# Conditioned two-stage block on one core: statistics of the first eight batch rows taken ahead, wider slot rows, and a new place for the third and fourth slot tile

## The chip, the core and the metric

The kernel runs on one core of a Trainium2 chip. The core has five engines with an instruction stream each: TensorE (PE, matmuls; its weight loads are a row of their own, PEld), VectorE (DVE), ScalarE (ACT), GpSimd (POOL) and SyncE (SP), which here only issues transfers. Each stream is executed in its own order and waits on semaphores. ACT and POOL issue transfers too; the instruction that issues one occupies the engine's stream. The metric is the device time of one execution in microseconds (us).

## The reference

All data is float32. The inputs are `x` (32 batch rows of 128 tokens of 512 features), a condition `t` (32 x 512), a mask (32 x 128) and the weights.

```python
shift, scale, gate = split(silu(t) @ ada_w + ada_b, 3)
norm = layernorm(x) * (1 + scale) + shift, zero where not mask
x = x + gate * where(mask, fwd(norm) + bwd(norm), 0)      # each: gelu(u @ w1 + b1) @ w2 + b2
shift2, scale2, gate2 = split(silu(t) @ ffada_w + ffada_b, 3)
ff = gelu_tanh((layernorm(x) * (1 + scale2) + shift2) @ ff_w1 + ff_b1) @ ff_w2 + ff_b2
out = x + gate2 * ff
```

The two halves of the first stage act on each token alone, so they are one product with a hidden layer of 1024. The mask is set for the *padding*, at most a quarter of the tokens, so the first stage is needed for few tokens.

## The kernel before, in words

**First stage on slots.** The masked tokens are packed into 512 slots, four tiles of 128 (`xc[0]` to `xc[3]`). Their numbers come from small matmuls on the mask (`find_slots`, L250), and POOL gathers their rows of `x` (`gather_slots`, L254). Each slot's scale, shift and gate are rows of a small matrix `mod1` (32 rows each), spread to the slots by matmuls of 32 x 512 (`slot_part`, L288): part 1 is scale, part 0 shift, part 2 gate. `mod1` itself comes from `modulation_matmuls` (L260) on the transposed condition. A slot tile is normalised and modulated on VectorE (`statistics` L149, `modulated` L166), transposed by TensorE and copied back by ScalarE (`transposed_slots`, L175). Tiles 0 and 1 together go through the hidden layer (`hidden`, L182: eight blocks of 4 matmuls with 256 columns, each ended by a GELU on ScalarE) and through the output layer (`project`, L196, one call for each tile); then `finish_slots` (L296) adds bias, gate and `x` and stores the rows into the DRAM scratch `x1_rows`. Tiles 2 and 3 follow in the same way at L1155 to L1200.

**Second stage on all tokens.** The 32 batch rows are taken in four pairs of sides; a pair is eight batch rows, a side four. For pair 0, `x` is loaded whole (L520), then `take_first_half` (L670) lets POOL gather the finished slot rows from `x1_rows` over the masked tokens, one indirect transfer per batch row; unmasked tokens keep `x`. Then come layernorm statistics (`Statistics`, L693), normalising, and a transposition: of side 0 by VectorE in 32 x 32 blocks and by 16 transfers (`turned`, L738) with ScalarE scaling afterwards (`scaled`, L747); of side 1 by TensorE (`transposed`, L730), called between the matmuls of `project` of tile 3. Both feed-forward products are done with seven block products in place of eight (`FirstProduct` L813, `SecondProduct` L1014), for which VectorE forms sums of weight blocks (`Weights.combine` L313, `weight_sums` L568) and of token blocks (`TokenBlocks.one`, L768). Some weight sums are stored in DRAM (`store_weight_sums`, L580) and loaded again (`load_weights`, L847). After pair 0's first matmul (L1210) the pairs run one after the other, and the next pair's gathers and statistics are put between the matmuls of the present one.

**What sets the order.** From L360 to L1362 the order in each stream is written by hand (`manual_schedule`): program order is stream order. SP's loads are issued in the order of the text: `ada_w` (3 MB), `w1` (2 MB) and `w2` (2 MB) behind the first gathers (L473 to L476), `ff_w1` (2 MB), `ffada_w` (3 MB), the broadcast biases, `ff_w2` (2 MB) and last `x` of pair 0 (2 MB, L520). On VectorE, between the statements named above, stand `count_more` (L585), the four combines of `ff_w1` (L620), `weight_sums` 1, 2, 3 and 4 (L624, L628, L633, L667) and the combines of `ff_w2` (L635).

## Time and profile before

| | us |
|---|---|
| median of three runs | 464.28 |
| lowest and highest | 462.79, 465.20 |
| profiled execution: span from its first to its last instruction | 463.6 |
| TensorE busy | 448.9 (97%) |
| VectorE busy | 330.6 (71%) |
| ScalarE busy | 175.7 (38%) |
| GpSimd busy | 159.8 (34%) |
| first hidden-layer matmul of slot tiles 0 and 1 (L188) | at 20.93 |
| last matmul of `project` of tile 1 ends (L203) | at 51.99 |
| first hidden-layer matmul of tiles 2 and 3 (L188) | at 57.94 |
| first matmul of pair 0's first product (L906) | at 87.27 |
| first matmul of the second product (L1093) | at 133.01 |

The page of the profile gives busy time by engine, the span in 40 slices of 11.6 us, and the costliest groups of instructions. The timeline of an engine lists its instructions in order; behind an instruction stands in brackets how long the engine sat idle before it, and what ended that. A float32 matmul with full precision is two instructions in these lists: `po_s` of L203, one `project`, is 8 matmuls and shows as x16. Matmuls overlap their successors, so their listed length is longer than the distance between two starts (592 ns against 430 ns for 512 columns, 379 ns against 216 ns for 256).

### The profile page before, as it was taken

The numbers are of one execution on the slowest core, as the hardware profiler recorded it, in microseconds if no ns is written. First come the engines' busy times: TensorE is split into PE (matmuls) and PEld (weight loads), VectorE is DVE, ScalarE is ACT, GpSimd is POOL, SyncE is SP. The second block draws the span as 40 slices with busy tenths as digits, with TensorE's granted clock in tenths as the row PEclk, the third lists the DMA queues.
The fourth block names the chain that finished last, engine by engine and source line by source line (L and its number), as shares of the span: only waits on it lengthen the run. The fifth ranks groups of instructions, "written<-read, shape, count | busy, mean of one in ns | idle before, by whom it ended". The sixth has DMA issues, their size and how long they took to land.

```text
span 463.6 us, 5827 instructions
## 1 busy us (share of the span) xinstructions
PE 448.9 (97%) x2000; PEld 364.4 (79%) x2000; DVE 330.6 (71%) x538; ACT 175.7 (38%) x380; POOL 159.8 (34%) x153
## 2 busy tenths in 40 slices
PE   6899999998999999999999999999999999999995
PEld 2475385676788888888888888888888887888884
DVE  4649778998669739996787498957963985433645
...
GB/s 280 386 408 364 322 107 95 219 326 104 85 5 211 97 102 105 354 90 113 1 229 113 68 169 310 99 81 34 212 105 60 155 142 79 81 74 109 0 81 105
DMA packets 82419, 70.42 MB, mean 152 GB/s; under 512 B 63168, under 2 KB 63696, under 8 KB 81362
## 3 DMA queue, kind: packets, MB, share of 16 engines
...
## 4 chain that ended last, share of the span: by engine, by line
PE 72%; DVE 8%; DMA 5%; SPq 4%; POOL 4%; issue 3%; ACT 3%; POOLq 0%; ACTq 0%; DVEq 0%
PE a_o L1093 17%; PE a_m L906 14%; PE e_o L1093 13%; PE e_m L906 11%; PE ph_s L188 6%; PE po_s L203 6%; SPq L745 4%; DMA x<-in_x_dram 2%; POOL x L674 1%; DMA xc<-in_x_dram,token_i_s 1%; DMA tw<-t_rows 1%; ACT xT L728 1%; PE part_s L283 1%; POOL ha L957 1%; PE pm_f L263 1%
## 5 line engine op out<-in xcount | busy, mean ns | idle before, releaser
L957 POOL TENSOR_TENSOR ha<-p_m,ha 128x512 f32<-128x512 f32 x20 | 26.2, 1311 | 151.9 <-ACT ha L964 142.0
L1093 PE MATMUL e_o<-fw,ha 128*128 128x256 f32 x256 | 57.9, 379 | 0.0
L728 ACT ACTIVATE xT<-xT,modT 128x128 f32<-128x128 f32 x112 | 44.0, 480 | 31.9 <-DMA xT<-xn 31.9
L1093 PE MATMUL a_o<-t,hb 128*128 128x256 f32 x240 | 54.1, 379 | 0.0
L1093 PEld LDWEIGHTS e_o<-fw,ha 128*128 128x128 f32 x256 | 48.6, 190 | 6.6
L1093 PEld LDWEIGHTS a_o<-t,hb 128*128 128x128 f32 x240 | 45.6, 190 | 6.2
L674 POOL DMA_INDIRECT x<-x_rows,slot_i x32 | 38.1, 1192 | 30.1 <-DMA x_rows<-t_s 18.0
L868 ACT ACTIVATE hb<-hb,biasT 128x256 f32<-128x256 f32 x64 | 29.0, 500 | 29.1 <-POOL hb L990 19.3
L957 POOL TENSOR_TENSOR hb<-p_m,hb 128x512 f32<-128x512 f32 x20 | 29.3, 1464 | 18.9 <-DVE sx L835 18.6
L920 ACT COPY p_m<-e_m 128x512 f32<-128x512 f32 x27 | 15.8, 586 | 47.9 <-PE e_m L906 47.9
L964 ACT COPY ha<-e_m 128x512 f32<-128x512 f32 x32 | 18.5, 578 | 28.6 <-PE e_m L906 26.6
L931 DVE TENSOR_TENSOR e_m<-a_m,ha 128x512 f32<-128x512 f32 x20 | 14.0, 698 | 21.6 <-POOL ha L957 9.5
L188 PE MATMUL ph_s<-xT_s,w 128*128 128x256 f32 x128 | 28.6, 381 | 0.5 <-issue 0.5
L1093 PE MATMUL a_o<-t,s 128*128 128x256 f32 x128 | 28.9, 379 | 0.0
L1093 PE MATMUL a_o<-fw,ha 128*128 128x256 f32 x128 | 28.9, 379 | 0.0
L1093 PE MATMUL e_o<-fw,s 128*128 128x256 f32 x128 | 28.9, 379 | 0.0
L203 PE MATMUL po_s<-w,h_s 128*128 128x512 f32 x64 | 28.6, 592 | 0.0
L188 PEld LDWEIGHTS ph_s<-xT_s,w 128*128 128x128 f32 x128 | 24.0, 190 | 5.2 <-ACT h_s L192 1.5
L1093 PEld LDWEIGHTS a_o<-t,s 128*128 128x128 f32 x128 | 24.3, 190 | 3.3
L1093 PEld LDWEIGHTS e_o<-fw,s 128*128 128x128 f32 x128 | 24.3, 190 | 3.3
L1093 PEld LDWEIGHTS a_o<-fw,ha 128*128 128x128 f32 x128 | 24.3, 190 | 3.3
L868 ACT ACTIVATE ha<-e_m,biasT 128x256 f32<-128x256 f32 x48 | 20.1, 468 | 16.2 <-PE e_m L906 10.5
...
## 6 DMA issues: line engine op xcount, KB each, us to landing
...
```

Source lines behind the costliest of these rows:

```text
L188: nc.tensor.matmul(ph[:, :n], w[:, k, ts(f, P)], xT[:, k, :], start=(k == 0), stop=(k == KC - 1))
L203: nc.tensor.matmul(po, h[f][:, ts(i, P)], w[:, f, :], start=(f == 0), stop=(f == HC - 1))
L674: nc.gpsimd.indirect_dma_start(out=xs[i // G][i % G // 2][:, i % 2], out_offset=None, in_=x1_rows[:slots, :], in_offset=bass.IndirectOffse ...
L728: nc.scalar.activation(out, src, AF.Identity, bias=shift, scale=scale)
L745: queues[b % len(queues)].dma_start(dst[ts(q, R), b], src[ts(b, R), q])
L868: nc.scalar.activation(dst[:, n], src[:, n], AF.Gelu_apprx_tanh, bias=biasT[:, f : f + 1])
L906: nc.tensor.matmul(bank[:, ts(n, QT)], self.w_block(j, product)[:, ts(n, P)], self.x_block(j, product), start=(product in ("P1", "P5") and ...
L920: nc.scalar.copy(p5, e)
L931: nc.vector.tensor_tensor(e, a, p5, add)
L957: nc.gpsimd.tensor_tensor(self.place(RESULT[j], c), self.p5[j], other, ALU.add)
L964: nc.scalar.copy(self.place(RESULT[j], c), src)
L1093: nc.tensor.matmul(part, src[:, k, ts(i, P)], w[product][:, k, :], start=(last and k == 0), stop=True, skip_group_check=True,)
```

## The change

It does the following.

- *Opening.* The bias of `mod1` and the bias rows of the hidden layers are loaded from ScalarE's queue in place of POOL's. The slots of tiles 2 and 3 are found before the last of the four blocks of the scale and shift matmuls. The gate part of `mod1` is computed as four independent products side by side in one bank, which are then added up by one more matmul with a 0/1 matrix (`strips`). Tiles 0 and 1 have statistics of their own each, and the first three hidden blocks are computed for tile 0 (128 columns) before tile 1 is transposed, then for tile 1.
- *Loads.* `x` of pair 0 goes ahead of `w2`, the two output biases of the first stage ahead of `ff_w1`.
- *Statistics ahead.* The tiles of `x` of pair 0 are two columns wider; VectorE writes mean and 1/deviation of each token there (`own_statistics`), POOL the power. The rows that `finish_slots` stores for tiles 0 and 1 carry the same two columns, into a second scratch `x1_wide`, and pair 0's gathers read from it. `Statistics` is not used for pair 0 any more.
- *Bias and x joined.* For tiles 0 and 1, `x + gate * bias` is formed ahead (`with_gated_bias`), so `finish_slots` has one multiplication and one addition before its statistics.
- *Tiles 2 and 3.* Their scale and shift rows, their modulation and their transposes go from between the first hidden blocks to behind `project` of tile 1, beside the modulation of the second stage; their gates go between the first and second hidden block of tiles 2 and 3.
- *VectorE's order.* `weight_sums` 1 and 2 go behind that too, normalising of side 0 to hidden block 4, `weight_sums(4)` and the normalising of side 1 to block 7, the combines of `ff_w2` and `fb2_step` behind the token block sum. The transfers of `turned` are issued in four groups between hidden blocks, each spread over both queues, and TensorE's transposes of side 1 stand in `project` of tile 2.

```diff
+    def own_statistics(t, n, name):
+        for i in range(n):
+            st = stp.tile([P, 6], F32, tag="st", name=f"st_{name}_{i}")
+            row = t[:, i]
+            nc.vector.bn_stats(st, row[:, :D])
+            nc.vector.bn_aggr(row[:, D : D + 2], st)
+        var = t[:, :, D + 1]
+        nc.vector.tensor_scalar(var, var, EPS, None, ALU.add)
+        nc.gpsimd.tensor_tensor(var, var, half[:, :n], ALU.pow)
...
+            for g in (after or {}).get(f, ()):
+                g()
...
+    def with_gated_bias(at, gate):
+        t = tp.tile([P, D], F32, tag="t", name=f"bg_s_{at}")
+        nc.vector.tensor_tensor(t, b2, gate, ALU.mult)
+        nc.vector.tensor_tensor(xc[at], xc[at], t, ALU.add)
     def finish_slots(at, h1, gate):
-        t = gated(project(at % (NC // 2), h1, w2, f"s{at}"), b2, gate, f"s_{at}")
-        nc.vector.tensor_tensor(t, t, xc[at], ALU.add)
-        nc.sync.dma_start(x1_rows[ts(at, P), :], t)
+        t = tp.tile([P, 1, D + 2], F32, tag="t", name=f"t_s_{at}")
+        row = t[:, 0, :D]
+        nc.vector.tensor_tensor(row, project(at, h1, w2, f"s{at}"), gate, ALU.mult)
+        nc.vector.tensor_tensor(row, row, xc[at], ALU.add)
+        own_statistics(t, 1, f"s_{at}_x1")
+        nc.sync.dma_start(x1_wide[ts(at, P), :], t[:, 0])
+        nc.sync.dma_start(x1_rows[ts(at, P), :], row)
...
-    broadcast_rows(modb_a, ada_b, nc.gpsimd)
     half = const.tile([P, G], F32, name="half")
     nc.vector.memset(half, -0.5)
+    strips = ssm.tile([P, B], F32, name="strips")
+    nc.vector.tensor_reduce(
+        strips, ident.rearrange("p (a b) -> p b a", b=B), axis=AX.X, op=ALU.add
+    )
...
+    broadcast_rows(modb_a, ada_b, nc.scalar)
...
-    load_behind_gathers(w1[:, :, :D], ssm_w1)
-    load_behind_gathers(w1[:, :, D:], bwd_w1)
-    load_behind_gathers(w2[:, :KC], ssm_w2)
-    load_behind_gathers(w2[:, KC:], bwd_w2)
-        nc.gpsimd.dma_start(
+        nc.scalar.dma_start(
...
-    modulation(pm, mod1, ada_a, modb_a, 0, 2)
-    gather_slots(find_slots(1, (ps_h, "h")))
-    rows = [(slot_part(c, 1, ps_o, "o"), slot_part(c, 0, ps_h, "h")) for c in range(2)]
-    pm = ps_o.tile([P, 512], F32, tag="o", name="pm_g")
...
-    mv, rstd = statistics(xc[:2], "s01")
-    xn_s = [
-        modulated(
-            xc[c], *rows[c], f"s{c}", xn[:, c], (mv[:, c, 0:1], rstd[:, c : c + 1])
-        )
-        for c in range(2)
-    ]
-    modulation_matmuls(pm, ada_a, 2, 3, range(KC))
...
-    for t, vec in ((b2, ssm_b2), (b2b, bwd_b2), (modb_f, ffada_b), (fb2, ff_b2)):
-        broadcast_rows(t, vec, nc.sync)
-    nc.sync.dma_start(fw2, ff_w2.rearrange("(k p) f -> p k f", p=P))
-    x_of = {0: load_x(0)}
-    transposed_slots(xn_s[0], xT_s[:, :, ts(0, P)], "s0")
-    transposed_slots(xn_s[1], xT_s[:, :, ts(1, P)], "s1")
...
+    gather_slots(find_slots(0))
+    load_behind_gathers(w1[:, :, :D], ssm_w1)
+    load_behind_gathers(w1[:, :, D:], bwd_w1)
+    raw = [x_tile(2 * n, 2) for n in range(2 * G // 2)]
+    x_of = {0: [[t[:, :, :D] for t in raw[2 * side : 2 * side + 2]] for side in range(2)]}
+    for n, t in enumerate(raw):
+        nc.sync.dma_start(t[:, :, :D], x[2 * n : 2 * n + 2].rearrange("b s d -> s b d"))
+    load_blocks(w2[:, :KC], ssm_w2)
+    load_blocks(w2[:, KC:], bwd_w2)
+    pick_slots(1)
...
+    modulation_matmuls(pm, ada_a, 0, 2, range(KC - 1))
+    gather_slots(find_slots(1, (ps_h, "h")))
+    modulation_matmuls(pm, ada_a, 0, 2, range(KC - 1, KC))
+    modulation_rows(pm, mod1, modb_a, 0, 2)
+    rows = [(slot_part(c, 1, ps_o, "o"), slot_part(c, 0, *((ps_o, "o"), (ps_h, "h"))[c])) for c in range(2)]
...
+    xn_s = [modulated(xc[c], *rows[c], f"s{c}", xn[:, c]) for c in range(2)]
...
+    for t, vec in ((b2, ssm_b2), (b2b, bwd_b2)):
+        broadcast_rows(t, vec, nc.sync)
+    nc.sync.dma_start(fw1, ff_w1.rearrange("(k p) f -> p k f", p=P))
+    ada_f = load_ada(ffada_w, "f", 3 * D)
+    for t, vec in ((modb_f, ffada_b), (fb2, ff_b2)):
+        broadcast_rows(t, vec, nc.sync)
+    nc.sync.dma_start(fw2, ff_w2.rearrange("(k p) f -> p k f", p=P))
...
+        if c == 0:
+            ph_s[f] = ps_h.tile([P, 512], F32, tag="h", name=f"ph_s0_{f}")
+        for k in range(KC):
+            nc.tensor.matmul(
+                ph_s[f][:, ts(c, P)],
+                w1[:, k, ts(f, P)],
+                xT_s[:, k, ts(c, P)],
+                start=(c == 0 and k == 0),
+                stop=(k == KC - 1),
+                skip_group_check=True,
...
+    transposed_slots(xn_s[0], xT_s[:, :, ts(0, P)], "s0")
+    gate_parts = tp.tile([P, D], F32, tag="t", name="gate_parts")
+    pm = ps_o.tile([P, 512], F32, tag="o", name="pm_g")
+    for k in range(KC):
+        nc.tensor.matmul(
+            pm[ts(k, B), :], sT[:, k, :], ada_a[:, k, ts(2, D)], start=True, stop=True
+        )
+    nc.scalar.copy(gate_parts, pm)
...
+    hidden_of_tile(0, 0)
+    pm = ps_o.tile([P, 512], F32, tag="o", name="pm_gate")
+    nc.tensor.matmul(pm[ts(2, B), :], strips, gate_parts, start=True, stop=True)
+    modulation_rows(pm, mod1, modb_a, 2, 3)
+    hidden_of_tile(1, 0)
+    transposed_slots(xn_s[1], xT_s[:, :, ts(1, P)], "s1")
+    hidden_of_tile(2, 0)
...
+    total, start_at, more_i, col_l = count_more()
+    for n, t in enumerate(raw):
+        own_statistics(t, 2, f"x_{n}")
     h1 = []
-    gs = []
-    xn_s = []
-    for c in range(2):
-        h1 += hidden(xT_s, NH, w1, 0, AF.Gelu, "s0", ssm, range(4 * c, 4 * c + 3))
-        if c == 0:
-            total, start_at, more_i, col_l = count_more()
-        gs.append(keep_gate(c, slot_part(c, 2, ps_o, "o")))
-        rows = slot_part(2 + c, 1, ps_o, "o"), slot_part(2 + c, 0, ps_o, "o")
-        xn_s.append(modulated(xc[2 + c], *rows, f"s{2 + c}", xn[:, 2 + c]))
-        if c == 0:
-            Weights(fw1, KC // 2, FF // 2, t_1).combine(0, 1, 2, 3)
-        h1 += hidden(xT_s, NH, w1, 0, AF.Gelu, "s0", ssm, range(4 * c + 3, 4 * c + 4))
-        if c == 1:
-            transposed_slots(xn_s[0], xT_t[:, :, ts(0, P)], "s2")
-    weight_sums(1)
+    for f in range(3):
+        hidden_of_tile(f, 1)
+        t = ssm.tile([P, NH], F32, tag="h", name=f"h_s0_{f}", bufs=HC)
+        nc.scalar.activation(t, ph_s[f][:, :NH], AF.Gelu, bias=biasT[:, f : f + 1])
+        h1.append(t)
+    gs = [keep_gate(c, slot_part(c, 2, ps_o, "o")) for c in range(2)]
+    mv_t, rstd_t = statistics(xc[2:], "s23")
     nc.vector.tensor_tensor(b2, b2, b2b, ALU.add)
     b2_row = dram.tile([1, D], F32, name="b2_row")
-    nc.sync.dma_start(b2_row, b2[0:1, :])
-    weight_sums(2)
+    for c in range(2):
+        with_gated_bias(c, gs[c])
+    Weights(fw1, KC // 2, FF // 2, t_1).combine(0, 1, 2, 3)
+    h1 += hidden(xT_s, NH, w1, 0, AF.Gelu, "s0", ssm, range(3, HC))
     finish_slots(0, h1, gs[0])
-    transposed_slots(xn_s[1], xT_t[:, :, ts(1, P)], "s3")
     t = in_blocks(group_of_tiles("tw_3"))
     t_sum[3] = [t[:, :4], t[:, 4:]]
     weight_sums(3)
...
+    store_weight_sums(3)
     nc.vector.tensor_scalar(modb_f[B : 2 * B], modb_f[B : 2 * B], 1.0, None, ALU.add)
     finish_slots(1, h1, gs[1])
-    store_weight_sums(3)
+    nc.sync.dma_start(b2_row, b2[0:1, :])
+    rows = [(slot_part(2 + c, 1, ps_o, "o"), slot_part(2 + c, 0, ps_h, "h")) for c in range(2)]
...
-    modulation(pm, mod2, ada_f, modb_f, 0, 3)
+    modulation_matmuls(pm, ada_f, 0, 3, range(KC))
+    xn_late = ssm.tile([P, 2, D], F32, tag="xT", name="xn_s_late", bufs=2)
+    for c in range(2):
+        t = modulated(
+            xc[2 + c], *rows[c], f"s{2 + c}", xn_late[:, c], (mv_t[:, c, 0:1], rstd_t[:, c : c + 1])
+        )
+        transposed_slots(t, xT_t[:, :, ts(c, P)], f"s{2 + c}")
+    modulation_rows(pm, mod2, modb_f, 0, 3)
...
-    gs = [
-        keep_gate(2, slot_part(2, 2, ps_o, "o")),
-        keep_gate(3, slot_part(3, 2, ps_h, "h")),
-    ]
+    weight_sums(1)
...
-    ptr = ps_t.tile([P, 512], F32, tag="tr", name="ptr_mod")
...
+    def transposed_modulation():
...
+    def second_gates():
+        gs[:] = [
+            keep_gate(2, slot_part(2, 2, ps_o, "o")),
+            keep_gate(3, slot_part(3, 2, ps_o, "o")),
+        ]
...
-    nc.vector.tensor_tensor(fb2_step, fb2[:, D // 2 :], fb2[:, : D // 2], ALU.subtract)
-    weight_sums(4)
+    fw2_of = Weights(fw2, HC // 2, D // 2, t_2)
...
+                out=raw[i // 2][:, i % 2] if p == 0 else xs[i // G][i % G // 2][:, i % 2],
                 out_offset=None,
-                in_=x1_rows[:slots, :],
+                in_=x1_rows if p else x1_wide,
...
-        for b in range(P // R):
+        for b in which:
             for q in range(P // R):
-                queues[b % len(queues)].dma_start(dst[ts(q, R), b], src[ts(b, R), q])
+                queues[(b + q // 2) % len(queues)].dma_start(dst[ts(q, R), b], src[ts(b, R), q])
...
-    take_first_half(0, x_of[0], range(G + 1))
-    store_weight_sums(1, queue=nc.gpsimd)
-    stats = [Statistics(x_of[0][side], f"0_{side}") for side in range(2)]
+    take_first_half(0, x_of[0], range(2 * G))
+    store_weight_sums(1)
     xT = [new_xT(0, side) for side in range(2)]
-    for i in range(G):
-        stats[0].one(i)
-    stats[0].root()
-    take_first_half(0, x_of[0], range(G + 1, 2 * G))
...
-    for i in range(G):
-        t = stats[0].normalised(i, xn[:, :, i])
-        nc.vector.transpose(t, t)
-    h1 = hidden(xT_t, NH, w1, 0, AF.Gelu, "s1", ssm)
-    turned(xn, xT[0], (nc.sync, nc.scalar))
+    def normalised_of_side_0():
+        for i in range(G):
+            t = normalised(raw[i // 2][:, i % 2], xn[:, :, i])
+            nc.vector.transpose(t, t)
...
+    def normalised_of_side_1():
+        t = sp.tile([P, G, D], F32, tag="s12", name="xn_0_1")
+        for i in range(G):
+            xn_b.append(normalised(raw[2 + i // 2][:, i % 2], t[:, i]))
...
+    def turn_rows(b):
+        return lambda: turned(xn, xT[0], (nc.sync, nc.scalar), (b,))
+    after = {4 + b: [turn_rows(b)] for b in range(4)}
+    after[0] = [second_gates, transposed_modulation]
+    after[1] = [lambda: weight_sums(2)]
+    after[4].insert(0, normalised_of_side_0)
+    after[7] += [lambda: weight_sums(4), normalised_of_side_1]
+    h1 = hidden(xT_t, NH, w1, 0, AF.Gelu, "s1", ssm, after=after)
     nc.scalar.activation(warm, biasT[0:1, 0:1], AF.Gelu_apprx_tanh)
     for k in range(KC):
         scaled(0, xT[0], k)
-    for i in range(G):
-        stats[1].one(i)
-    stats[1].root()
-    xn_b = []
-    for c in range(2):
...
-    po_s2 = project(0, h1, w2, "s2")
...
-    between = {0: turn(0), 1: turn(1), 2: keep_and_turn, 4: turn(3)}
-    po = project(1, h1, w2, "s3", between, (ps_h, "h"))
-    store_weight_sums(4, 2)
+    po_s2 = project(0, h1, w2, "s2", {2: turn(0), 4: turn(1), 6: turn(2), 7: turn(3)})
     of_x[0] = TokenBlocks(0, xT)
     of_x[0].one(1)
+    fw2_of.combine(0, 1)
+    nc.vector.tensor_tensor(fb2_step, fb2[:, D // 2 :], fb2[:, : D // 2], ALU.subtract)
+    with_bias(2, po_s2)
+    with_gate(2, gs[0])
+    with_x(2)
+    po = project(1, h1, w2, "s3", bank=(ps_h, "h"))
+    store_weight_sums(4, 2)
     with_bias(3, po)
     with_gate(3, gs[1])
```

## The prediction

> **What bounds the kernel now.** I read the page first, then TensorE's timeline up to 135 us, VectorE's for the same stretch, and last who waits for whom behind pair 0's first product. Parts 1 and 2 of the page:
>
> ```profile
> PE 448.9 (97%) x2000; PEld 364.4 (79%) x2000; DVE 330.6 (71%) x538; ACT 175.7 (38%) x380; POOL 159.8 (34%) x153
> ...
> PE   6899999998999999999999999999999999999995
> ```
>
> TensorE is the bound nearly everywhere. Only slices 0 and 8 and the tail have room, so an edit pays only if it takes TensorE's own work away, or idle time in those places. TensorE's timeline of the opening (start, length, idle before it):
>
> ```profile
> 12.86 1.99 PE L283 MATMUL part_s<-mod,pick 32*128 32x512 f32 x8 [0.15 <-DVE mod L273]
> 14.78 3.62 PE L263 MATMUL pm_g<-ada_a,sT 128*32 128x512 f32 x8
> 18.33 0.66 PE L179 MATMUL ptr_s<-ident,xn_s 128*128 128x128 f32 x4
> 19.55 0.66 PE L179 MATMUL ptr_s<-ident,xn_s 128*128 128x128 f32 x4 [0.56 <-DVE xn_s L172]
> ...
> 20.93 5.42 PE L188 MATMUL ph_s<-xT_s,w 128*128 128x256 f32 x24 [0.49 <-issue]
> ...
> 34.48 1.13 PE L283 MATMUL part_s<-mod,pick 32*128 32x512 f32 x6
> ...
> 52.08 3.63 PE L263 MATMUL pm_f<-ada_f,sT 128*32 128x512 f32 x24
> 55.64 1.98 PE L283 MATMUL part_s<-mod,pick 32*128 32x512 f32 x4
> ```
>
> From 20.93 to 98 us the timeline lists no idle time over 0.3 us. Two things matter. The gate product (14.78) is done while the slot rows are still on their way, so it costs nothing now. And a gate, scale and shift that stand together share 1.13 us (34.48: three matmuls on different rows of the array, side by side), while two gates alone take 1.98 us (55.64: same rows, one after the other).
>
> VectorE's timeline, for the two loads that it waits for:
>
> ```profile
> 14.30 0.69 DVE L155 BATCH_NORM_STATS2 st_s<-xc 128x6 f32<-128x512 f32 x1 [0.48 <-DMA xc<-in_x_dram,token_i_s]
> ...
> 32.82 1.22 DVE L317 TENSOR_TENSOR t<-fw 128x1024 f32<-128x1024 f32 x1 [2.35 <-DMA fw<-in_L_cond_ff_w_dram]
> ```
>
> Waits from 87 to 125 us (total, times, longest):
>
> ```profile
> POOL x L674 <- DMA x<-in_x_dram: 4.2, 1, 4.2
> ...
> DVE e_m L931 <- POOL ha L957: 2.9, 2, 1.8
> ...
> PE e_m L906 <- DVE e_m L931: 2.1, 3, 1.3
> ```
>
> This is slice 8: POOL waits for pair 1's `x`, then issues its gathers, and a sum that VectorE and TensorE need stands behind them. From 98 to 124 us TensorE is idle 3.25 us (22.75 busy of 26.00).
>
> **Two rules of the Trainium skill.** "TensorE: Matmul & The Clock Gate", Part 1, says that TensorE runs at half clock until a few microseconds of steady work, and falls back after an idle window of about 3.4 us. The trace shows the first half: the 512-column matmuls `pm_ss` last between 592 and 1062 ns, the later `pm_g` 592 to 617. After the change TensorE has no gate product to fill 14.8 to 17 us; the gap is under 2 us, so I go on full clock and keep the other as a rival. The same page, "Back-to-back issue gap", says that matmuls of 128 columns are spaced by their weight loads rather than by their columns. That would hit the new half blocks. The row at hand disagrees: the float32 `pl_s` of 12.01 us, 128 columns, start 0.112 us apart, half of the 0.216 us of 256 columns. I go by the trace.
>
> **The change, in four stretches of TensorE's time.**
>
> *1. To the first hidden matmul, 20.93 us before.* The gather of tile 0 still lands at 14.30: its slots are found no sooner. With statistics of its own a tile takes 2.63 us from statistics to modulated (tile 2 before: 27.85 to 30.48), so tile 0 is ready at 16.93, not 17.99. Transposes and copy take 1.34 us (19.50 to 20.84 for tile 1): 18.27. TensorE meanwhile does the four transposes (0.44), the gate product as four side by side (0.86, a quarter of 3.44) and the small transposes (0.3): 16.95 + 1.6 = 18.6. `w1`'s first half was issued at 10.56 and landed 7.0 us later, 17.6, so it doesn't bind. Start at 18.6, **2.3 us earlier**. The bias loads moved to ScalarE's queue (six issues of about 0.5 us) fall before its first copy at 19.02, where it sat idle 12 us. The `mod1` bias may land a microsecond later than the 10.05 before, which delays the second gathers' search, but that was at 12.75 and has until about 17.
>
> *2. From there to the end of `project` of tile 1, 31.06 us before.* Added: the summing matmul 0.86 (one `project` is 6.87 for eight), tile 1's transposes, which were ahead of the start, 0.44; the 48 half matmuls at 0.112 for 24 at 0.216, 0.2. The two groups of three go (2 x 1.06 net) and the two gates alone come (1.91 net). The transposes of tiles 2 and 3 leave (0.88). Sum +0.4: 31.5 us, end at 50.1 (before 51.99).
>
> VectorE must keep up. After `count_more` (24.3) it has eight rows of `x` at 0.80 (72.29 to 73.07 before) and four additions, 7.0 us; the loads of `x` now land where `w2` did, by 24 to 27, so no wait: 31.3. Statistics of tiles 2 and 3: 33.1. Output biases: all loads run at about 0.385 MB/us behind each other; `ff_w1` landed at 32.8 with 10.2 MB ahead of or in it; with 0.5 MB more the biases land at 34.2. Four operations of 0.73 and the bias sum: 37.9. `ff_w1` has 2.6 MB more ahead: 39.6; four combines of 1.26: 44.6. `finish_slots(0)` (5 operations, 2.5): 47.1; `weight_sums(3)` 49.2; the bias row 49.6 (it lands at 48.2: 16.1 MB). So VectorE is ready for `finish_slots(1)` 0.5 us before it is due. I cost this at nothing, but the cover is thin; every microsecond by which `ff_w1` is later is paid. POOL's powers stand on no queue that is waited for then.
>
> *3. From there to pair 0's first product, 35.28 us before.* Added: four scale and shift matmuls for tiles 2 and 3, 1.99 (row 12.86), and their transposes, 0.88. The gates and the transposes of the modulation only change places. A new wait: the hidden layer of tiles 2 and 3 needs their modulated rows, which stand on VectorE behind `finish_slots(1)`. From TensorE's end: 0.36 to start, two operations 1.5, statistics 1.0, two tiles of 1.5, then transposes and copy 1.34: 7.2 us. TensorE's own work is 1.99 + 3.44 + 0.88 = 6.3, with switches 6.5: 0.7 us idle. Sum 38.9, so the first product starts at 89.0, not 87.27: **+1.7 us**. The gathers and transfers have cover: eight gathers from about 56.5 at 1.4 each, the fourth landed at 63.5, normalising from 64 (behind `weight_sums(2)`) to 69, the 16 transfers to 80, 16 scalings of 0.39 to 87. SP's half of them shares the queue with nothing due.
>
> *4. Behind it.* The hand-made order is the same. But `with_x(2)`, and SP's stores of weight sums 4 and 2 queued behind its store, were issued 2.1 us before the first product and now come 0.3 before it, since VectorE does the token sum (1.22), two combines (2.5) and `fb2_step` (0.4) first. The reload of weight sums 1 (6.8 us to landing, used 10.0 us after the first product) starts about 1 us later, at 3.0: just in time. The second reload still moves data when pair 1's `x` is issued at +9.2. I take 0.5 us, between 0 (SP's queue drains in time) and 1.8 (all of the shift), for the longer wait of POOL's gathers.
>
> Sum: -2.3 + 0.4 + 3.6 + 0.5 = **+2.2 us** on the profiled span of 463.6. The median is 0.7 above that span; 464.3 + 2.2 = 466.5.
>
> **Rivals.** A measurement can tell about 0.5%, 2.3 us, from no change.
>
> *VectorE becomes the bound* (slower still): loads come 2 us later than my count, because the broadcasts read one row 128 times. Then the combines end at 46.6, `finish_slots(1)` starts 1.5 to 2 us late, and the third stretch shifts with it: 468.5, up to 470.2. For it: the 0.5 us of cover. Against: `ff_w1` landed at the even rate before.
>
> *Loads come earlier* (not slower): with nothing else on POOL's queue the first gather lands at 13.3 or before and `ff_w1` by 38.6. The start moves to 17.7 (bound by `w1`), VectorE is no longer late for tiles 2 and 3 (-0.7), and pair 1's `x` isn't delayed (-0.5): 464.4. For it: the `mod1` bias shared POOL's queue. Against: the second gathers, with that bias long landed, took 5.5 us and more as well.
>
> *The idle time of slice 8 goes* (faster): at the first product ScalarE has finished scaling, which before ran 1.4 us into it. If the sums behind the gathers then ran early enough to hide all 3.25 us: about 461. Against: they wait for the gathers, not for ScalarE.
>
> *Half clock in the opening*: 3.4 us of the hidden layer at half speed, +1.7: 468.2. *The change doesn't do what it says*: the statistics of pair 0 would have to stand on the path to gain anything by leaving it. TensorE had no wait between 57.94 and 87.27, so they were hidden and their removal gains nothing; that is in the forecast.
>
> **Chances.** Forecast 0.42 (465.4 to 467.7), VectorE late 0.25, not slower 0.17, half clock 0.06, slice 8 gone 0.10. The range of 8 in 10 leaves out the faster case and the top of VectorE's: 462.5 to 470.2. Slower by over 0.5% (above 466.6): 0.25 + 0.06 + 0.19 of the forecast's 0.42 = 0.50. Within: 0.23 + 0.17 = 0.40. Faster: 0.10.
>
> **What would show it.** Right: the first hidden matmul at 18 to 19 us; `project` of tile 1 ending near 50; an idle piece of about 0.7 us ahead of the hidden layer of tiles 2 and 3, ended by a copy of ScalarE; first product at 88.5 to 89.5; idle from 98 to 124 as before or slightly more. Wrong: VectorE's combines waiting for `ff_w1` beyond 40; the first product before 87; or less than 2 us idle behind it.

## The result, and the profile after

| | us |
|---|---|
| before: median of four runs (lowest, highest) | 463.53 (462.61, 465.20) |
| after: median of four runs (lowest, highest) | 470.04 (469.58, 471.05) |
| ratio after to before, 95% interval | 1.0126 (1.0085 to 1.0167) |
| forecast, range | 466.5, 462.5 to 470.2 |

The kernel became slower, as forecast, but by 6.5 us and not by 2.2. In both profiled executions the time is the span and 1.6 to 1.7 us around it (465.20 and 463.6 before, 469.94 and 468.2 after). So the span shown of before belonged to the longest of its runs. The kernel before was therefore profiled once more in the course of the experiments; that execution took 461.95, with a span of 460.2. The four stretches of the prediction, from the timelines of TensorE:

| stretch | before | before, second profile | after | forecast | measured against the first (the second) |
|---|---|---|---|---|---|
| start to first hidden matmul | 20.93 | 21.33 | 19.70 | -2.3 | -1.2 (-1.6) |
| to the end of `project` of tile 1 | 31.06 | 31.06 | 32.71 | +0.4 | +1.7 (+1.7) |
| to pair 0's first product | 35.28 | 35.44 | 39.27 | +3.6 | +4.0 (+3.8) |
| to the second product | 45.74 | 42.81 | 46.94 | +0.5 | +1.2 (+4.1) |
| to the end | 330.6 | 329.6 | 329.6 | 0 | -1.0 (0) |
| span | 463.6 | 460.2 | 468.2 | +2.2 | +4.6 (+8.0) |

The page after, parts 1 and 2:

```profile
PE 452.0 (97%) x2026; PEld 368.4 (79%) x2026; DVE 335.4 (72%) x549; ACT 176.4 (38%) x381; POOL 157.9 (34%) x147
...
PE   6899999999799999999999999999999999999995
...
PEclk9899999999899999999999999999999999999999
```

TensorE is busy 3.1 us longer, with about the same work. PEclk, the granted clock, has an 8 in slices 1 and 10 (counted from 0). The first is the opening; TensorE's timeline there:

```profile
13.91 1.99 PE L299 MATMUL part_s<-mod,pick 32*128 32x512 f32 x8 [0.79 <-DVE mod L289]
17.16 0.66 PE L190 MATMUL ptr_s<-ident,xn_s 128*128 128x128 f32 x4 [1.27 <-DVE xn_s L183]
17.75 1.67 PE L577 MATMUL pm_g<-ada_a,sT 128*32 128x512 f32 x8
...
19.70 2.00 PE L564 MATMUL ph_s<-xT_s,w 128*128 128x128 f32 x8
21.63 1.04 PE L589 MATMUL pm_gate<-gate_parts,strips 128*32 128x512 f32 x2
22.61 1.16 PE L564 MATMUL ph_s<-xT_s,w 128*128 128x128 f32 x8
```

The same eight half-block matmuls take 2.00 us at 19.70 and 1.16 at 22.61. The windows view (bounds, then length and busy time of PE, PEld, DVE, ACT, POOL, then granted clock, DMA share, GB/s) has the granted clock beside it:

```profile
16.00:18.00 2.00, 0.84 (x8) 0.58 (x12) 1.57 (x4) 0.14 (x1) 0.33 (x1) 1.00 1.06 393
18.00:20.00 2.00, 2.00 (x11) 0.58 (x4) 1.51 (x3) 0.98 (x3) 0.57 (x1) 0.52 1.03 404
20.00:22.00 2.00, 2.00 (x9) 1.62 (x9) 0.19 (x1) 0.13 (x2) 0.00 (x0) 0.63 1.05 391
22.00:24.00 2.00, 2.00 (x14) 1.40 (x13) 0.69 (x1) 0.00 (x0) 0.00 (x0) 1.00 1.05 388
...
121.00:124.00 3.00, 3.00 (x9) 2.41 (x8) 0.88 (x2) 0.58 (x1) 2.82 (x3) 0.52 0.05 10
```

The trace's clock record has half clock from 18.08 to 21.49 and from 120.48 to 123.89, 3.41 us each. A slot of that length, busy and all at half speed, loses half of it, 1.7 us, where TensorE bounds. The third stretch, in the next part of TensorE's timeline:

```profile
52.50 1.99 PE L299 MATMUL part_s<-mod,pick 32*128 32x512 f32 x8
54.42 3.63 PE L279 MATMUL pm_f<-ada_f,sT 128*32 128x512 f32 x24
57.98 1.09 PE L190 MATMUL ptr_s<-ident,xn_s_late 128*128 128x128 f32 x8
59.86 1.99 PE L199 MATMUL ph_s<-xT_s,w 128*128 128x256 f32 x8 [0.78 <-ACT xT_s L191]
```

This is the prediction's account almost to the tenth: rows of 1.99, transposes, and 0.78 idle for ScalarE's copy (forecast 1.99, 0.88, 0.7). VectorE's timeline, for the cover that the prediction called thin:

```profile
39.53 1.23 DVE L342 TENSOR_TENSOR t<-fw 128x1024 f32<-128x1024 f32 x1 [0.34 <-DMA fw<-in_L_cond_ff_w_dram]
...
45.74 0.69 DVE L320 TENSOR_TENSOR t_s<-po_s,gs 128x512 f32<-128x512 f32 x1 [1.20 <-PE po_s L216]
...
52.61 0.69 DVE L320 TENSOR_TENSOR t_s<-po_s,gs 128x512 f32<-128x512 f32 x1 [1.80 <-PE po_s L216]
```

The combines waited for `ff_w1` until 39.53 (forecast 39.6), and VectorE then stood waiting for TensorE at both `finish_slots`. It was late at neither. Behind the first product (at 91.68), first SP's timeline, then POOL's, then TensorE's:

```profile
91.67 0.33 SPq L1255 DMA_DIRECT2D x_rows<-t_s  x1
...
101.95 2.43 SPq L351 DMA_DIRECT2D x<-in_x_dram  x4
```

```profile
108.76 1.83 POOL L733 DMA_INDIRECT x<-x_rows,slot_i  x1 [6.08 <-issue]
...
118.37 1.27 POOL L1025 TENSOR_TENSOR ha<-p_m,ha 128x512 f32<-128x512 f32 x1
```

```profile
120.43 2.06 PE L974 MATMUL e_m<-xn_sy,tw 128*128 128x256 f32 x4 [2.55 <-DVE e_m L999]
```

The store that heads SP's queue is level with the first product (before 2.1 us ahead of it); pair 1's `x` is issued 10.3 us behind the first product (before 9.2), POOL's six gathers end at 118.4 and TensorE waits 2.55 us for a sum behind them.

The 1.1 us by which `x` is issued later do not come from that store. On SP, `x` stands behind tile 3's rows, and these wait for the addition `with_x(3)` on VectorE. VectorE and POOL in the timeline of before, then of after:

```profile
95.38 0.69 DVE L1182 TENSOR_TENSOR t_s<-t_s,xc 128x512 f32<-128x512 f32 x1
...
95.46 1.73 POOL L957 TENSOR_TENSOR hb<-p_m,hb 128x512 f32<-128x512 f32 x1 [18.57 <-DVE sx L835]
```

```profile
99.42 1.58 POOL L1025 TENSOR_TENSOR hb<-p_m,hb 128x512 f32<-128x512 f32 x1 [26.91 <-DVE hb L1004]
...
99.80 1.75 DVE L1254 TENSOR_TENSOR t_s<-t_s,xc 128x512 f32<-128x512 f32 x1
```

Before, VectorE's addition began 0.08 us ahead of POOL's and took its usual 0.69. After, POOL's began 0.38 us ahead, and VectorE's took 1.75. The prediction has no such term; experiments 9 and 11 are about the mechanism. The same happens in experiments 1 to 5, 7, 8 and 12.

### The profile page after: what moved, and what is told of

The parts are those of the page before. It is cut to its first block, busy times and chain, and to the rows that moved or that the text cites. A ratio compares the mean times of both kernels' runs of the same rounds, so it can differ in the third digit from the quotient of the medians.

```text
span 468.2 us, 5888 instructions
## 1 busy us (share of the span) xinstructions
PE 452.0 (97%) x2026; PEld 368.4 (79%) x2026; DVE 335.4 (72%) x549; ACT 176.4 (38%) x381; POOL 157.9 (34%) x147
## 4 chain that ended last, share of the span: by engine, by line
PE 90%; DVE 3%; DMA 2%; POOL 2%; issue 1%; SPq 0%; ACT 0%; POOLq 0%; DVEq 0%; ACTq 0%
PE a_o L1161 23%; PE e_o L1161 18%; PE a_m L974 17%; PE e_m L974 13%; PE po_s L216 6%; PE ph_s L199 5%; DMA x<-in_x_dram 2%; PE ph_s L564 1%; PE part_s L299 1%; PE pm_ss L279 1%; POOL x L733 1%; PE pm_f L279 1%; PE last L1161 1%; DMA mask_u<-in_mask_BxS_bk_dram 0%; POOL xc L254 0%
## 5 line engine op out<-in xcount | busy, mean ns | idle before, releaser
L1161 PEld LDWEIGHTS a_o<-t,hb 128*128 128x128 f32 x240 | 45.6, 190 | 6.2
L733 POOL DMA_INDIRECT x<-x_rows,slot_i x24 | 28.7, 1194 | 11.9 <-issue 10.6
L974 PE MATMUL a_m<-xT,tw 128*128 128x256 f32 x96 | 24.6, 379 | 0.0
L1004 DVE TENSOR_TENSOR hb<-a_m,hb 128x512 f32<-128x512 f32 x20 | 13.7, 685 | 14.3 <-PE a_m L974 14.3
```

Source lines behind the costliest of these rows:

```text
L733: nc.gpsimd.indirect_dma_start(out=raw[i // 2][:, i % 2] if p == 0 else xs[i // G][i % G // 2][:, i % 2], out_offset=None, in_=x1_rows if ...
L974: nc.tensor.matmul(bank[:, ts(n, QT)], self.w_block(j, product)[:, ts(n, P)], self.x_block(j, product), start=(product in ("P1", "P5") and ...
L1004: nc.vector.tensor_tensor(dst, a, dst if prior else self.p5[j], add)
L1161: nc.tensor.matmul(part, src[:, k, ts(i, P)], w[product][:, k, :], start=(last and k == 0), stop=True, skip_group_check=True,)
```

## The experiments

All times are compared with runs of before on the same chip. The ratio in brackets, with its 95% interval, is estimated from the runs of both kernels; it is not the quotient of the two medians. Unless another kernel is named, an edit is made to the kernel after. "P1" is the start of pair 0's first product, "d" the stretch from there to the second product.

**1. The gate product again ahead of the transposes,** accumulated in one place, without `strips`.

```diff
-    transposed_slots(xn_s[0], xT_s[:, :, ts(0, P)], "s0")
-    gate_parts = tp.tile([P, D], F32, tag="t", name="gate_parts")
...
-    for k in range(KC):
-        nc.tensor.matmul(
-            pm[ts(k, B), :], sT[:, k, :], ada_a[:, k, ts(2, D)], start=True, stop=True
-        )
-    nc.scalar.copy(gate_parts, pm)
+    modulation_matmuls(pm, ada_a, 2, 3, range(KC))
+    transposed_slots(xn_s[0], xT_s[:, :, ts(0, P)], "s0")
+    modulation_rows(pm, mod1, modb_a, 2, 3)
```

> The changed kernel, with the gate part of the first modulation computed again as one accumulated product ahead of the transposes (3.4 us of matmuls where TensorE was idle from 15.9 to 17.2 us), and without the adding matmul (0.86). Theory A, half clock: TensorE stays at full clock from 18 to 21.5 us; the first hidden matmul starts later, near 20.5, but the first half block takes 0.9 instead of 2.0 us and 0.86 is saved behind it; pair 0's first product at about 90.5 instead of 91.7, the kernel 1.2 us faster than the changed one (near 468.8 in the median). Theory B, the clock doesn't matter there: the later start and the saved matmul cancel, first product at 91.5 to 91.9, no difference.

Measured: 469.61 (ratio 1.0123, 1.0075 to 1.0172). First hidden matmul at 20.52, P1 at 90.47 (after 91.68), no half clock in the opening, d 46.96. The product (3.62) and nothing after it stands in place of the side-by-side form and its sum (1.06 and 1.05 at full clock, experiment 2), some 1.5 us more work, and the first product still starts 1.2 us sooner: the side-by-side form saved TensorE work in a place where TensorE had to wait, and in the profile of after the wait cost it the clock.

**2. One unused matmul in the gap** of the opening; its result goes nowhere.

```diff
+    fill = ps_t.tile([P, 512], F32, tag="tr", name="fill")
+    nc.tensor.matmul(fill, ident, ada_a[:, 0, :D], start=True, stop=True)
```

> The changed kernel with one matmul more, whose result nobody reads: 128 columns of weights, 512 columns moved, put into the idle time behind the scale and shift rows of tiles 0 and 1 (15.9 us). Theory A, half clock: the filler keeps the clock up, the 3.4 us at half clock from 18.1 us are gone, pair 0's first product comes 1.5 to 1.9 us earlier (about 90.0), the kernel is 1.7 us faster than the changed one. Theory B: more work on the bound engine, 0 to 0.9 us slower, first product at 91.7 to 92.5.

Measured: 468.63 (1.0112, 1.0070 to 1.0154), P1 at 90.52, d 46.85. TensorE's timeline of this kernel:

```profile
16.22 1.12 PE L539 MATMUL fill<-ada_a,ident 128*128 128x512 f32 x2
...
18.14 1.06 PE L579 MATMUL pm_g<-ada_a,sT 128*32 128x512 f32 x8
...
19.38 1.16 PE L566 MATMUL ph_s<-xT_s,w 128*128 128x128 f32 x8
```

`pm_g` takes 1.06 us in place of 1.67 and the half block 1.16 in place of 2.00. P1 is 1.2 us earlier with more work done. There was no half clock behind P1 here either, and d stayed the same, so the second slot at half clock, at 120 us, cost nothing: POOL's chain sets the time there.

The whole times of experiments 1 and 2 do not tell them from the kernel after (1.0126): the 1.2 us are read from one profile of each. The mean clocks of the runs speak for the filler as well. They are 0.998 or more in five of the six runs of experiment 2, and in one of the four runs of the kernel after.

**3. The stores of weight sums sooner:** `with_x(2)` again ahead of the combines.

```diff
-    fw2_of.combine(0, 1)
-    nc.vector.tensor_tensor(fb2_step, fb2[:, D // 2 :], fb2[:, : D // 2], ALU.subtract)
     with_bias(2, po_s2)
     with_gate(2, gs[0])
     with_x(2)
+    fw2_of.combine(0, 1)
+    nc.vector.tensor_tensor(fb2_step, fb2[:, D // 2 :], fb2[:, : D // 2], ALU.subtract)
```

> The changed kernel with bias, gate and x of tile 2 put ahead of the two combines and the bias difference on VectorE, so that SP's stores of the slot rows and of weight sums 4 and 2 are issued about 2.8 us before pair 0's first product instead of level with it. First product unchanged, 91.7. Theory A (stores late, so pair 1's x late, so POOL's gathers late): pair 1's x lands about 1.1 us earlier against the first product, TensorE's idle time of 2.55 us before 120.4 falls to about 1.4, and if it falls far enough the half clock behind it (1.7 us) goes too: 1.1 to 2.8 us faster. Theory B (x is issued behind the last slot rows anyway, and its own 2 MB set its landing): within 0.3 us of the changed kernel.

Measured: 467.75 (1.0101, 1.0054 to 1.0148), d 45.56, that is 1.4 less. The store stands 2.8 us ahead of P1. Pair 1's `x` is issued 10.3 us behind P1 as in the kernel after, but its first tile lands 14.4 us behind P1 in place of 15.9. TensorE's longest wait behind P1 is 1.26 us, as in the profile of before, in place of 2.55.

P1 itself was at 92.31 in this profile, with half clock from 15.75 for 6.8 us.

**4. Tiles 2 and 3 back between the hidden blocks of tiles 0 and 1,** each gate beside a scale and a shift.

```diff
-    rows = [(slot_part(2 + c, 1, ps_o, "o"), slot_part(2 + c, 0, ps_h, "h")) for c in range(2)]
...
-    xn_late = ssm.tile([P, 2, D], F32, tag="xT", name="xn_s_late", bufs=2)
...
+    gs = [keep_gate(0, slot_part(0, 2, ps_o, "o"))]
+    xn_s = [tile_ahead(0)]
...
+    h1 += hidden(xT_s, NH, w1, 0, AF.Gelu, "s0", ssm, range(3, 7))
+    gs.append(keep_gate(1, slot_part(1, 2, ps_o, "o")))
+    xn_s.append(tile_ahead(1))
...
+    h1 += hidden(xT_s, NH, w1, 0, AF.Gelu, "s0", ssm, range(7, HC))
+    transposed_slots(xn_s[0], xT_t[:, :, ts(0, P)], "s2")
     finish_slots(0, h1, gs[0])
+    transposed_slots(xn_s[1], xT_t[:, :, ts(1, P)], "s3")
```

> The changed kernel with the scale and shift rows, the modulation and the transposes of slot tiles 2 and 3 back between the hidden blocks of tiles 0 and 1, each gate beside a scale and a shift; the statistics of pair 0's x follow tile 2's modulation on VectorE. Theory A (the new place costs TensorE's own time and a wait): the rows alone (1.9), the transposes there and the idle 0.8 go, the two groups of three cost 0.2 more than the gates alone: pair 0's first product 2.5 us earlier, near 89.2, the kernel 2.5 us faster. Theory B (VectorE, now with 3 us more ahead of finish_slots, becomes late): project of tile 1 no earlier, but its closing work 1 to 2 us later; the gain is under 1 us.

Measured: 467.44 (1.0087, 1.0064 to 1.0110), P1 at 88.86, 2.8 us sooner. This is the largest single part: the third stretch, of which the forecast said 3.6, is 3.8 us shorter, and the second, where the rows and transposes stand again, 1.0 longer. This profile, too, has half clock in the opening, for 3.4 us from 17.4.

**5. All three taken back** (1, 3 and 4 together).

> The changed kernel with three parts undone together: the gate product ahead of the transposes (as in the first experiment), the stores of tile 2 first (third), the rows, modulation and transposes of tiles 2 and 3 back (fourth). What is left of the change are the statistics taken ahead, the wider slot rows, bias and x joined, the order of the loads. Theory A (these three parts hold the whole loss, the rest was hidden before and is hidden now): pair 0's first product at 87.5 to 88.0, 45.6 us from there to the second product, the kernel within 0.3% of the one before (463.0 to 464.8). Theory B (the rest costs too, through VectorE's longer work and the later weights): first product at 88.7 or later, the kernel over 0.5% slower than before.

Measured: 465.77 (1.0054, 1.0035 to 1.0073). First hidden matmul at 21.61, P1 at 89.06, d 45.57. The theory of equality fell. What is left of the change still costs: the block of parts stands at 13.66 (before 12.86), since finding the slots of tiles 2 and 3 was put ahead of it, and the gate product waits for a bank that tile 0's shift rows now use:

```profile
13.66 1.99 PE L299 MATMUL part_s<-mod,pick 32*128 32x512 f32 x8 [0.79 <-DVE mod L289]
16.68 3.62 PE L279 MATMUL pm_g<-ada_a,sT 128*32 128x512 f32 x8 [1.03 <-DVE xn_s L182]
```

Part of this belongs to this one execution. In experiment 1, with the same order, the gate product did not wait: VectorE could begin tile 0's statistics at 13.53 there and only at 14.87 here, when the gathered rows had landed.

**6. The kernel before, with three of pair 1's four tiles of `x` loaded early,** right behind the block transfers of side 0.

```diff
     turned(xn, xT[0], (nc.sync, nc.scalar))
+    x_early = load_side(1, 0, spare)
+    x_late = [x_tile(f"{3 * G}")]
+    nc.sync.dma_start(x_late[0], x[3 * G : 3 * G + 2].rearrange("b s d -> s b d"))
...
```

> The kernel before, unchanged but for pair 1's x: three of its four tiles are loaded right behind the block transfers of pair 0's side 0 (at about 80 us, their buffers are free there) in place of behind the last slot rows at 96.5. First product unchanged at 87.3. Theory A (pair 1's x decides when POOL starts its gathers, and these hold up the sums behind them): gathers start at about 99.7, when the last slot rows have landed, in place of 103.1, TensorE's 3.2 us of idle time from 98 to 124 fall to under 1, the kernel is 2 to 3 us faster than before. Theory B (the gathers' own 1.3 us each and the slot rows decide): under 0.7 us faster.

Measured: 466.80 (1.0102, 1.0046 to 1.0157). The loads were early, but they ran into the block transfers, whose last part ScalarE and then TensorE now waited for. ScalarE's timeline of this kernel, and TensorE's:

```profile
86.78 5.50 ACT L728 ACTIVATE xT<-xT,modT 128x128 f32<-128x128 f32 x14 [3.95 <-DMA xT<-xn]
```

```profile
93.57 1.13 PE L906 MATMUL e_m<-xT,fw 128*128 128x256 f32 x4 [2.33 <-ACT e_m L952]
```

In the kernel before that scaling began at 82.44 (83.07 in its second profile). The gathers were no sooner either (102.90): POOL's two additions ahead of them, fed by the delayed TensorE, ended only at 102.7.

**7. Three taken back as in 5, the gate product in two halves around tile 0's transposes, and the early loads** of 6, which there come behind block transfers that start 5 us sooner.

```diff
-    modulation_matmuls(pm, ada_a, 2, 3, range(KC))
+    modulation_matmuls(pm, ada_a, 2, 3, range(2))
     transposed_slots(xn_s[0], xT_s[:, :, ts(0, P)], "s0")
+    modulation_matmuls(pm, ada_a, 2, 3, range(2, KC))
...
     h1 = hidden(xT_t, NH, w1, 0, AF.Gelu, "s1", ssm, after=after)
+    x_early = load_side(1, 0, spare)
+    x_late = [x_tile(f"{3 * G}")]
+    nc.sync.dma_start(x_late[0], x[3 * G : 3 * G + 2].rearrange("b s d -> s b d"))
...
```

> The three-parts-undone kernel with two additions: the gate product is split in halves around the transposes of tile 0, so that TensorE has work on both sides of them, and pair 1's x is loaded early as in the sixth experiment. Theory A: first hidden matmul at 19.8 instead of 20.5, pair 0's first product at about 87.0, 43 us from there to the second product, the kernel 2.5 to 3.5 us faster than the one before (460 to 461). Theory B (the opening is bound by loads, and the stall by the gathers themselves): within 1 us of the kernel before.

Measured: 462.23 (22 runs; 0.9984, 0.9968 to 1.0000). First hidden matmul at 19.93, P1 at 87.88, d 42.65. The opening and d came as theory A said. P1 was 0.9 us later, and the gain of 2.5 to 3.5 us did not come: the time is that of theory B. This is the fastest version of the study, and it is not clearly faster than before.

**8. The kernel before, with only the rows, the modulation and the transposes of tiles 2 and 3 moved** behind `project` of tile 1.

```diff
-        rows = slot_part(2 + c, 1, ps_o, "o"), slot_part(2 + c, 0, ps_o, "o")
-        xn_s.append(modulated(xc[2 + c], *rows, f"s{2 + c}", xn[:, 2 + c]))
...
+    rows = [(slot_part(2 + c, 1, ps_o, "o"), slot_part(2 + c, 0, ps_h, "h")) for c in range(2)]
...
+    xn_late = ssm.tile([P, 2, D], F32, tag="xT", name="xn_s_late", bufs=2)
+    for c in range(2):
+        t = modulated(
+            xc[2 + c], *rows[c], f"s{2 + c}", xn_late[:, c], (mv_t[:, c, 0:1], rstd_t[:, c : c + 1])
+        )
+        transposed_slots(t, xT_t[:, :, ts(c, P)], f"s{2 + c}")
```

> The kernel before with one part of the change alone: scale and shift rows, modulation and transposes of slot tiles 2 and 3 behind project of tile 1. Theory A (the new place costs TensorE's own time and a wait on VectorE): the rows alone 2.0, a wait of about 0.6, less 0.3 in the groups that become single gates: pair 0's first product at 89.3 to 89.8 instead of 87.3, the kernel 2 to 2.5 us slower than before. Theory B (TensorE finds room for them, as the modulation of the second stage and its transposes wait anyway): under 0.7 us slower.

Measured: 467.98 (1.0105, 1.0073 to 1.0138). From the first hidden matmul to P1 it takes 69.2 us (before 66.3): the move alone costs 2.9 us. P1 was at 90.76, later than my theory's number, in part because this profile also began late (first hidden matmul at 21.53). The store that heads SP's queue stands 2.1 us ahead of P1 as in before, and still `x` is issued 10.3 us behind P1: here, too, `with_x(3)` took 1.76 us beside POOL's addition.

**9. The kernel before, with two tiles of pair 1's `x` ahead of the block transfers.**

```diff
+    x_early = load_side(1, 0, spare)
     turned(xn, xT[0], (nc.sync, nc.scalar))
...
-    x_of[1] = load_x(1, spare)
+    x_of[1] = [x_early, load_side(1, 1)]
```

> The kernel before, with one edit: the first two of pair 1's four tiles of x are loaded ahead of the block transfers of side 0, not behind pair 0's first product; the other two stay where they were. In the earlier try three tiles stood behind those transfers and delayed their landing by 4 us. Theory A (only the collision took the gain): the tiles wait for the stores of weight sums that free their buffers (about 68.5 us) and land by about 72, before the block transfers start at 72.4; the first product stays at 87.3 to 87.8, POOL's gathers start near 100 to 101 (they still need tile 3's stored rows) and the stretch from there to the second product falls from 45.7 to 43 or less: 2 to 3 us faster than before, ratio 0.994 to 0.996. Theory B (the transfers of x hold up the block transfers wherever they stand ahead of the first product): block transfers land 2 us or more later, TensorE waits at the first product again, and the time is within 0.3% of before or slower.

Measured: a median of 467.58 (1.0036, 1.0008 to 1.0063), but a median says little here: of 22 runs 7 lie between 461.9 and 464 at a mean clock of 0.998 or more, and 12 above 467 at 0.990 to 0.996. The collision was gone, as theory A said: ScalarE's scaling began at 83.05. The gathers ended earlier, too, and that brought a stall that neither theory had. VectorE's timeline of this kernel, then POOL's, then TensorE's:

```profile
109.11 4.04 DVE L845 TENSOR_TENSOR xT<-xT,xn_sy 128x512 f32<-128x512 f32 x1
```

```profile
108.88 1.28 POOL L957 TENSOR_TENSOR ha<-p_m,ha 128x512 f32<-128x512 f32 x1
110.11 1.27 POOL L957 TENSOR_TENSOR hb<-p_m,hb 128x512 f32<-128x512 f32 x1
111.33 1.26 POOL L986 TENSOR_TENSOR ha<-ha 128x512 f32<-128x512 f32 x1
```

```profile
114.94 2.08 PE L906 MATMUL a_m<-sx,tw 128*128 128x256 f32 x4 [3.69 <-DVE hb L936]
```

An addition that takes 0.69 us elsewhere took 4.04: it began 0.2 us behind POOL's first addition and ended 0.6 us behind the third. TensorE stood for 3.69 us and then ran at half clock for 6.8.

**10. The kernel before once more,** unchanged.

> The kernel before once more, unchanged, for a second profile of it. Theory A (the profiled execution that the prediction was summed on was one of its slower ones, by the landing of the opening's gathers and loads): the span is 461 to 462.5 and most of the difference to 463.6 lies ahead of the first hidden matmul (20.93) or ahead of pair 0's first product (87.27). Theory B (the spread arises later): these starts agree within 0.3 us and the difference lies behind 133 us.

Measured: one execution of 461.95, span 460.2. Neither theory fits: the starts agree within 0.6 us with the first profile (21.33, P1 87.83, later if anything), and most of the difference lies between P1 and the second product: d is 42.81, not 45.74 (another 1.0 us lies behind it). Pair 1's `x`, issued 9.2 us behind P1 in both, let the first gather go 5.1 us after its issue in place of 6.6, and the six gathers took 1.0 to 1.5 us each where two of the first profile took 1.77 and 2.09. POOL's timeline of the first profile, then of the second:

```profile
106.58 2.09 POOL L674 DMA_INDIRECT x<-x_rows,slot_i  x1 [0.31 <-issue]
...
112.85 1.27 POOL L957 TENSOR_TENSOR ha<-p_m,ha 128x512 f32<-128x512 f32 x1
```

```profile
104.90 1.00 POOL L674 DMA_INDIRECT x<-x_rows,slot_i  x1 [0.30 <-issue]
...
110.47 1.28 POOL L957 TENSOR_TENSOR ha<-p_m,ha 128x512 f32<-128x512 f32 x1
```

From 98 to 124 us TensorE is idle 1.22 us here and 3.25 in the first profile. So the idle time that the prediction read off the profile (its "slice 8"; the digit is that of slice 9, counted from 0) is mostly absent from a shorter run of the same kernel.

**11. Experiment 9 with the seventh gather ahead of POOL's additions.**

```diff
-            put(2, 6, take_first_half, p + 1, x_next, range(G, G + 2))
-            put(3, 4, take_first_half, p + 1, x_next, range(G + 2, G + 3))
+            if p == 0:
+                put(2, 6, take_first_half, p + 1, x_next, range(G, G + 3))
+            else:
+                put(2, 6, take_first_half, p + 1, x_next, range(G, G + 2))
+                put(3, 4, take_first_half, p + 1, x_next, range(G + 2, G + 3))
```

The later pairs keep their order.

> The previous kernel (before, with two tiles of pair 1's x loaded ahead of the block transfers) with one more edit: POOL issues the seventh of pair 1's gathers ahead of its additions to ha and hb, not behind them. In the previous kernel's profile the gathers ended at 108.9, POOL's three additions ran from 108.88 to 112.59, and VectorE's addition xT<-xT,xn_sy, begun at 109.11, took 4.04 us instead of 0.69; TensorE waited 3.7 us and then went to half clock for 6.8 us. Theory A (VectorE's addition of two operands from on-chip memory cannot run beside POOL's additions, and the one that comes second waits): POOL's additions now begin at 110.2 or later, VectorE's additions are over by 110, every one lasts 0.7, no half clock, the stretch from the first to the second product is 42.7 to 43.2, and the times no longer fall into two groups: 461.5 to 462.5, ratio 0.995 to 0.997. Theory B (the long addition had another cause, such as the transfers of x): it stays long in the profile, or the times stay in two groups around 462 and 467.7.

Measured: 462.71 (0.9995, 0.9979 to 1.0011), all 22 runs between 461.9 and 465.7 at a mean clock of 0.997 or more, d 42.67, no half clock. POOL's additions began at 110.93, and VectorE's took their usual time. VectorE's timeline of this kernel:

```profile
109.36 0.68 DVE L845 TENSOR_TENSOR xT<-xT,xn_sy 128x512 f32<-128x512 f32 x1
```

Theory A's mechanism is shown: one gather put ahead, which moves POOL's additions by 2 us, takes the long addition and the two groups away. Its gain did not come: the time is that of before within the interval (median 462.86 of 43 on this chip). That before's own stall is small in most of these runs would explain it; no profile of such a run shows it.

**12. The kernel after with early `x`,** loaded as in 7.

```diff
     h1 = hidden(xT_t, NH, w1, 0, AF.Gelu, "s1", ssm, after=after)
+    x_early = load_side(1, 0, spare)
+    x_late = [x_tile(f"{3 * G}")]
+    nc.sync.dma_start(x_late[0], x[3 * G : 3 * G + 2].rearrange("b s d -> s b d"))
...
```

> The kernel after, with one edit: three of pair 1's four tiles of x are loaded behind the block transfers of side 0, in place of 10 us behind the first product. Theory A (all that the kernel after loses behind the first product is pair 1's later x, through POOL's gathers): the stretch from the first to the second product falls from 46.9 to 42.7 to 43.2, as in the version with three parts taken back, and the first product stays within 1 us of 91.7; time about 466, ratio 1.004 to 1.007. Theory B (the later stores and reloads of weight sums hold TensorE up as well): the stretch stays at 44.5 or more, with TensorE waiting for ScalarE's p_m behind the reload, and the time is 467.5 or more.

Measured: 466.98 (1.0089, 1.0066 to 1.0112), d 43.93, P1 at 90.35. Of the 4.1 us by which d of after exceeds that of the second profile of before, 3.0 went with the early `x`. The rest, 1.1, lies ahead of POOL's first addition behind the six gathers, 23.77 us behind P1 in place of 22.64. TensorE's wait of 0.65 us for `p_m`, which theory B named, is there, but experiment 7 has it as well with d at 42.65, so it does not explain the rest. The runs lie between 464.3 and 470.5, the longest ones at a mean clock of 0.993.

## Why the prediction was right in sign and short in size

**Stretch 1** was to gain 2.3 us and gained 1.2. The term that failed is the rival that I held at 0.06: half clock in the opening. The prediction put "the gap is under 2 us, so I go on full clock". The gap was 1.27 us, as short as that, and TensorE was busy for 2.2 of the 3.4 us ahead of the fall. The time lost by arithmetic is 0.8 us of 1.6 ahead of the first hidden matmul and 0.9 of 1.8 behind it. Experiments 1 and 2, which fill the gap, both have P1 1.2 us sooner, and so has experiment 12 (1.3), whose profile has the gap but not the half clock. The rest (0.3) has two parts. TensorE's own chain from tile 0's transposes to the first hidden matmul takes 1.8 us at full clock (experiments 2 and 12), where the forecast had 1.6. And tile 0 was modulated at 17.11, not at 16.93, as VectorE had to wait for its power on POOL:

```profile
16.36 0.75 DVE L183 SCALAR_TENSOR_TENSOR xn_s<-xn_s,rstd_s,part_s 128x512 f32<-128x512 f32 x1 [0.54 <-POOL rstd_s L160]
```

Finding the slots of tiles 2 and 3 was put ahead. The power could have begun at 15.01; POOL's two gathers for these tiles, begun at 13.52, held it up to 15.73. The prediction counted that search as free because it lay ahead of 17 us, and did not ask what would be queued behind it.

**Stretch 2** was to cost 0.4 and cost 1.7. The second half of the half-clock slot is 0.9 of the missing 1.3. The term for the summing matmul, 0.86, was near (1.04 long, 0.98 to the next start). The trace's spacing for matmuls of 128 columns was right: at full clock those of a half block start 0.111 to 0.112 us apart (experiment 5), as forecast. (The Trainium skill, "TensorE: Matmul & The Clock Gate", section "Back-to-back issue gap", which the prediction sets against it, has the spacing set by the weight load and the matmul together.) The other 0.4 is there at full clock, too: in experiments 2 and 12 the stretch is 0.8 us longer than before. It has not been traced further.

**Stretch 3** was to cost 3.6 and cost 4.0 (3.8 against the second profile). The mechanism and the size are confirmed from both sides. The move of tiles 2 and 3 as a whole was forecast at 2.5 (3.6 here, less the 1.1 that left stretch 2): experiment 4 takes 2.8 us back, experiment 8 adds 2.9 to the kernel before. That VectorE would be in time, with loads landing at 39.6, was right, and so the rival in which it becomes the bound did not happen.

**Stretch 4** was to cost 0.5, between 0 and 1.8, and cost 1.2 in the two profiles that the prediction compares. Its mechanism was right: experiment 3, which takes back only the order on VectorE and so puts the stores sooner, gave 1.4 back. The size was short, since I took 0.5 in the hope that part of the shift would vanish in the queue.

The fourteen profiles say how a delay is passed on. In the twelve whose POOL order is the original one and in which VectorE isn't held at the gathers' end, d is the time from P1 to POOL's first addition behind the six gathers plus 20.1 to 20.3 us: 25.58 and 45.74 before, 22.64 and 42.81 in its second profile, 26.69 and 46.94 after, 26.19 and 46.36 in experiment 6. So whatever delays that addition is paid in full. What delays the start of the gathers is not. In the kernel after and in experiments 1, 2 and 4 the first gather begins 16.0 to 17.8 us behind P1; in all four it ends at 18.9, and the addition begins at 26.7. The first gather in POOL's timelines of experiments 1 and 4 (P1 at 90.47 and 88.86):

```profile
108.22 1.15 POOL L722 DMA_INDIRECT x<-x_rows,slot_i  x1 [6.75 <-issue]
```

```profile
104.84 2.92 POOL L744 DMA_INDIRECT x<-x_rows,slot_i  x1 [4.99 <-issue]
```

In experiments 3, 5 and 8 two gathers are through by 18.9, and the addition begins at 25.4, one gather (1.3 us) sooner. So the delay was paid in steps of a gather; what holds the gathers until then is not shown. The later issue of `x` alone does not put d above that of before's first profile: experiments 3, 5 and 8 issue it 10.3 us behind P1 as well, and have d of 45.6.

**The base** was the second miss. I set the sum on the span and then said that "the median is 0.7 above that span". A run's own time is 1.6 us above its span, so the profiled execution was one of 465.2, above the median. That hid part of the price of stretch 4. The kernel after and the three experiments with its order there all have 26.7 us to the first addition. Before has 25.6 in one profile and 22.6 in the other, and these are the ends of its runs: 465.20 is the longest of the first four, 461.95 is shorter than all 27 runs of before that stand beside it. A usual run of before seems to lie between: 31 of the 43 runs beside experiment 11 are below 463.8, and 12 of the 27 beside experiment 9. No profile shows one. The median difference of 6.5 us lies between the 4.6 of the first pair of profiles and the 8.0 of the second.

**Rivals.** "VectorE late" would have given 468.5, up to 470.2, by a mechanism that wasn't there. That the median, 470.04, still lies just inside the range is luck, as the top of the range was set for that rival. "Loads earlier" failed, as `ff_w1` landed at the forecast time; "slice 8 gone" is the wrong way round, as the stall grew; "half clock" was right and too cheaply held. That the statistics of pair 0 were hidden and their removal gains nothing fits the result: the third stretch has all its forecast additions and no gain beside them.

**What stays open.** Why the fall to half clock comes in one execution and not in another is not settled. The kernel of experiment 12 has the same opening, with the same idle pieces of 0.79 and 1.27 us, and ran it at full clock. TensorE's timeline of this kernel:

```profile
17.38 0.67 PE L190 MATMUL ptr_s<-ident,xn_s 128*128 128x128 f32 x4 [1.27 <-DVE xn_s L183]
17.98 1.06 PE L577 MATMUL pm_g<-ada_a,sT 128*32 128x512 f32 x8
```

The two falls of after are exactly thirty slots of 3.413 us apart (18.08 and 120.48), which speaks for fixed slots. But the busy share of a slot does not decide alone. In both kernels the gap lies whole within one slot, and TensorE is busy for 2.15 us of it in after and for 2.14 in experiment 12. I laid the slots of the clock records over all fourteen profiles. The three slots at full clock with less than 1.2 us of work were all followed by half clock. Of eleven with 1.9 to 2.2 us three were, and these are the openings of after and of experiments 3 and 4, with 1.2 us or more of the work in matmuls of 32 rows. No experiment moved the gap, or the kind of work in it, on purpose. And the fastest version (experiment 7) has not been shown to beat before.
